# Zero points in packed 16-bit form, GpSimd makes the weights, VectorE takes half of the rescales

## The chip, the core and the metric

The kernel runs on one core of a Trainium2 chip. The metric is the device time of one execution in microseconds (us); of several runs the median is given. Besides that there is a profile of one execution, with the start and duration of every instruction of each engine: TensorE (PE, its weight loads PEld), VectorE (DVE), ScalarE (ACT), GpSimd (POOL) and SyncE (SP), which here only issues DMAs.

## What is computed

The input is 2 x 1024 rows of 1024 floats, 2048 rows in all. Each goes through a "macaron": half a feed-forward layer, a state-space layer (a long convolution along the 1024 values), and the same feed-forward layer again. Only the feed-forward layer matters here. Its three weight matrices are stored with 4 bits a value, eight to a 32-bit word, with a scale and a 4-bit zero point for every group of 128 input rows:

```python
w = (qw[:, None, :] >> shifts[None, :, None] & MAXQ).reshape(-1, qweight.shape[1])
z = ((qz[:, :, None] >> shifts[None, None, :] & MAXQ) + 1).reshape(qzeros.shape[0], -1)
W = (w - z[g_idx]) * scales[g_idx]
h = jax.nn.silu(xf @ Wg) * (xf @ Wu)
out = h @ Wd
```

Wg and Wu have 1024 rows (8 groups) and 2752 columns, Wd has 2752 rows (22 row blocks, 21 zero and scale rows) and 1024 columns. The result is `x + 0.5 * ffn(layernorm(x))`.

## The kernel before

**Jobs.** The rows are cut into four blocks b of 512. A feed-forward layer of one block is a job, and eight jobs (two per block) run one after the other. Only job 0 (j = 0) makes the weights: it unpacks them, writes them to DRAM as whole floats (`w_q`, `wd_q`), and all jobs load tiles from there. So nearly all that follows happens in job 0.

**Gate and up.** The 2752 columns are cut into units of 128 columns of gate or of up, and these into eight waves: five of six units, two of four, and a last one of five. For every wave eight steps g run over the groups of 128 input rows. In a step TensorE multiplies the weight tile (128 rows, 768 columns in a wave of six) with two parts of the normalized rows, a float part and a 16-bit rest, and adds both into the unit's accumulator in PSUM. Between two steps the accumulator is multiplied by the ratio of two scales (`scaled`, L521), so that it always stands in the scale of the next group; the last ratio is held by itself and goes into the gating. ScalarE does this (L523) or VectorE (L525). In `gate_up` L569 decides: ScalarE takes the even units, and in job 0 also the unit at place 1 of the wave, so four of six. After step 7 `gated` applies silu (L581, ScalarE), multiplies gate by up (hf, L584, VectorE), and splits the product into two parts on GpSimd: hh (L586) and hl (L588). There are two hf buffers and six accumulators.

**Down.** Two halves a of 512 output columns; in each 22 steps f over 128 rows with four accumulators. L628 decides who rescales: ScalarE takes c = 0 and 2, and in job 0 also c = 1 in three of four steps.

**Making the weights.** `fetch` (L407) loads a wave's packed words, `fetch_zeros` (L414) its zero points, one bf16 each, repeated for 16 partitions. `bytes_of` (L421) turns the words into two tiles of bytes with two VectorE instructions: the even nibbles by a mask, the odd ones by a shift and a mask. A byte then holds a nibble from 0 to 15. `dequantize` (L433) makes one of the eight tiles of a wave: VectorE takes every fourth byte, subtracts the zero point, and writes floats (L438); SP writes the tile to `w_q` (L442). For wave 0, GpSimd also copies each tile's first 16 partitions into the first weight tile by its own DMA (L441), so that step 0 need not go through DRAM. `fetch_down`, `split_down` and `dequantize_down` (L446 to L474) do the same for down, six blocks of eight tiles of 512 columns. The zero points themselves are unpacked once by `zero_points` (L257) and stored in DRAM. The dequantized tiles and the weight tiles of the steps share one ring of eight buffers (`wpool`), loads run four steps ahead (`AHEAD`).

**What sets the order.** Each engine works off its own list in order, and SP is one such list, with tile writes and weight loads mixed. The Tile framework's planner orders the instructions from the program text. Hooks set where in the text a piece of weight making stands (`first_weights`, L476: wave w's fetch 3 steps, its split 1 step ahead of its first tile, which stands 12 steps before the wave), and `in_order_of_writing` keeps some of them in the order written. `start` (L1277) writes out the beginning by hand: loads, zero points, moments of the rows, wave 0's tiles, transposes.

Of the kernel before, what the change touches and what calls it, by code (L numbers as in the profile page):

```python
# [12 lines left out]
I32 = mybir.dt.int32  # L13
U8 = mybir.dt.uint8
F32R = mybir.dt.float32r
# [21 lines left out]
STEPS = [(w, g) for w in range(len(WAVES)) for g in range(GK)]  # L37
NH = HID // 512
LIFT = 2.0**20
NST = 64  # L40
# [12 lines left out]
def macaron_s4_kernel(  # L53
# [180 lines left out]
    s_dn = const.tile([P, NC, GD], F32, tag="s_dn", name="s_dn")  # L234
    z_dram = dpool.tile([2 * GK, INTER], BF16, tag="z", name="z_dram")
    zd_dram = dpool.tile([GD, HID], BF16, tag="zd", name="zd_dram")
    ok = const.tile([P, 8], F32, tag="ok", name="ok")
# [19 lines left out]
    def zero_points(which, z):  # L257

        p, n = z.shape
        zi = t2(f"zi_{which}").bitcast(I32)[:p, : 8 * n]  # L260
        for k in range(8):
            nc.vector.tensor_scalar(
                zi.rearrange("p (a k) -> p k a", k=8)[:, k, :],
                z,
                4 * k,
                15,
                ALU.logical_shift_right,
                ALU.bitwise_and,
            )
        tab = t2(f"ztab_{which}").bitcast(BF16)[:p, : 8 * n]  # L270
        nc.vector.tensor_scalar(tab, zi, 1.0, None, ALU.add)
        dst, seg, queue = (zd_dram, SEGD, nc.sync) if which else (z_dram, SEG, nc.scalar)
        queue.dma_start(dst.rearrange("g (s n) -> (g s) n", s=seg), tab)
# [15 lines left out]
    def scales(k0, k1, row):  # L289
# [9 lines left out]
        if k1 == WIDE:  # L299
# [13 lines left out]
        nc.vector.tensor_scalar(  # L313
            own[:, :, GK - 1 :], s[:, :, GK - 1 :], 1.0 / LIFT, None, ALU.mult
        )

    def scales_down():
# [16 lines left out]
        )  # L334
        nc.vector.tensor_scalar(ratd[:, :, GD - 1 :], s_dn[:, :, GD - 1 :], 0.5, None, ALU.mult)

# [67 lines left out]
    packed = {}  # L404
    NIBBLES = 0x0F0F0F0F

# [7 lines left out]
    def fetch_zeros(w):  # L414
        z = t2(f"z_{w}").bitcast(BF16)[:, : width_of(w)]
        for own, i, lo, hi in columns(w):
            src = z_dram[GK * i : GK * i + GK, lo:hi]
            nc.sync.dma_start(z[:, own], src.unsqueeze(1).to_broadcast([GK, 16, hi - lo]))
        packed[w][1] = z

    def bytes_of(raw, even):  # L421

        nc.vector.tensor_scalar(even, raw, NIBBLES, None, ALU.bitwise_and)
        nc.vector.tensor_scalar(raw, raw, 4, NIBBLES, ALU.logical_shift_right, ALU.bitwise_and)
        view = lambda a: a.bitcast(U8).rearrange("p (n k) -> p k n", k=4)
        return view(even), view(raw)

    def split(w):
        raw = packed[w][0]
        even = t4(f"even_{w}").bitcast(I32)[:, : width_of(w)]  # L430
        packed[w][0] = bytes_of(raw, even)

    def dequantize(w, j):  # L433

        parts, z = packed[w]
        q = wpool.tile([P, width_of(w)], F32R, tag="w", name=f"q_{w}_{j}")
        src = parts[j % 2][:, j // 2, :]
        nc.vector.tensor_tensor(q, src, z, ALU.subtract)  # L438
        dst = w_q[w].rearrange("(r j) n -> j r n", j=8)[j]
        if w == 0:  # L440
            nc.gpsimd.dma_start(first_tile[j:P:8].bitcast(F32), q[: P // 8].bitcast(F32))  # L441
        nc.sync.dma_start(dst, q.bitcast(F32))  # L442
        if j == 7:
            packed.pop(w)

    def fetch_down(a, rt):  # L446
# [4 lines left out]
        nc.sync.dma_start(both[:, 0], down_qw[rt * P : rt * P + n, cs])  # L451
        z = t4(f"zd_{a}_{rt}").bitcast(BF16)[:n, :512]
        g0 = 8 * rt
# [8 lines left out]
    def split_down(a, rt):  # L462
        both, z = packed[a, rt]
        packed[a, rt] = (bytes_of(both[:, 0], both[:, 1]), z)

    def dequantize_down(a, rt, j):
        parts, z = packed[a, rt]
        n = z.shape[0]
        q = wpool.tile([P, 512], F32R, tag="w", name=f"qd_{a}_{rt}_{j}")[:n]
        nc.vector.tensor_tensor(q, parts[j % 2][:, j // 2, :], z, ALU.subtract)  # L470
        rows = wd_q[a][8 * P * rt : 8 * P * rt + 8 * n]
        nc.sync.dma_start(rows.rearrange("(r j) n -> j r n", j=8)[j], q.bitcast(F32))
        if j == 7:
            packed.pop((a, rt))  # L474

    def first_weights(up, dn, at):  # L476


        for w in range(1, len(WAVES)):
            s0 = 8 * w - 12  # L480
            if w > 1:
                both = lambda w=w: (fetch(w), fetch_zeros(w))
                at(up, s0 - 3, lambda both=both: in_order_of_writing(both, ET.SP))
                at(up, s0 - 1, lambda w=w: in_order_of_writing(lambda: split(w), ET.DVE))
            else:
                at(up, 0, lambda: in_order_of_writing(lambda: split(1), *STARTING))
            for j in range(8):
# [39 lines left out]
    def gate_up(j, b, hooks):  # L527
# [3 lines left out]
        for s, (wi, g) in enumerate(STEPS):  # L531
# [17 lines left out]
            for k, pos, done in turns:  # L549
# [18 lines left out]
                if g < GK - 1:  # L568
                    on_act = unit % 2 == 0 or (j == 0 and pos == 1)  # L569
                    if unit == 2 * WIDE:  # L570
# [35 lines left out]
    def down(j, b, hooks):  # L606
# [3 lines left out]
        for d, (a, f) in enumerate(steps):  # L610
# [7 lines left out]
            for c in range(4):  # L618
                for k, part in enumerate(reversed(h[f])):
# [7 lines left out]
                    )  # L627
                on_act = c % 2 == 0 or (j == 0 and c == 1 and f % 4 < 3)  # L628
                if f < GD - 1:
# [647 lines left out]
    def start():  # L1277
# [19 lines left out]
        moments(0, 1, then)  # L1297
        deviations(0, 1, -LIFT)
        for i in range(8):
            dequantize(0, i)  # L1300
# [100 lines left out]
```

## Time and profile before

| | us |
|---|---|
| Median of 3 runs (lowest to highest) | 2210.38 (2209.15 to 2211.67) |
| The profiled execution | 2211.56 |
| Its span, first to last instruction | 2209.8 |
| PE busy | 2121.7 (96%) |
| VectorE busy | 1703.2 (77%) |
| ScalarE busy | 1425.0 (64%) |
| GpSimd busy | 367.8 (17%) |
| First multiplication with weights | 28.75 |
| End of job 0, about | 333 |

A line of a group of instructions names the source line, the engine, the operation, output and inputs with their shapes, and the count; then the busy time and the mean duration in ns, then the idle time of the engine just ahead of them and what ended it. A line of the timeline gives start and duration in us, the same names, and in brackets the idle time ahead with its releaser. A busy PE is not a PE at its full pace: matmuls are pipelined, and the granted clock is given apart (1.00 is full). The pace is best read from the start of a step to the start of the next.

### The profile page before, as it was taken

Reading aid. Unit: us, or ns where it says so; the run is one execution under the profiler, and the core shown is the slowest. Engines: PE = TensorE matmul, PEld = TensorE weight load, DVE = VectorE, ACT = ScalarE, POOL = GpSimd, SP = SyncE. Lnnn points to the kernel's source line nnn. Section 1 sums busy time; section 2 is a strip of 40 time slices with the busy share of each in tenths; the row PEclk is TensorE's granted clock in tenths of the full one; section 3 lists DMA queues with packets and bytes.
Section 4 is the critical chain, followed back from the end, with each engine's and each line's share of the span. In section 5 each row is a group of like instructions: output and inputs, shape, how many; then the busy total and the mean of one; then the engine's idle time right before and its main releaser. Section 6 shows DMA issues by size and latency. Waiting matters only on the chain.

```text
span 2209.8 us, 27967 instructions
## 1 busy us (share of the span) xinstructions
PE 2121.7 (96%) x9524; PEld 1416.0 (64%) x9524; DVE 1703.2 (77%) x2803; ACT 1425.0 (64%) x2245; POOL 367.8 (17%) x389
## 2 busy tenths in 40 slices
PE   5888899999999999999999999999999999999998
PEld 3454575566867658655685558676586765865576
DVE  7777968777886877778877788867788677777776
ACT  5667776555764577666766667646776467766775
POOL 0222301121011220122102220112201122012210
PEclk9999999999999999999999999999999999999999
DMA  7778774434443545544655454434445354554443
GB/s 247 249 244 281 235 249 155 133 110 155 136 153 116 171 138 155 193 143 121 205 170 167 125 172 138 153 115 157 134 138 153 115 177 137 154 195 143 133 131 121
DMA packets 163669, 359.93 MB, mean 163 GB/s; under 512 B 22395, under 2 KB 27572, under 8 KB 163518
## 3 DMA queue, kind: packets, MB, share of 16 engines
q1 hardware_dynamic: 162670, 356.50, 50.7%
q8 instruction: 78, 1.28, 0.2%
q10 hardware_dynamic: 592, 1.16, 0.1%
q0 software_dynamic: 256, 0.39, 0.1%
q14 instruction: 73, 0.60, 0.1%
HBM read 306.86 MB, written 50.73 MB: 162 GB/s over the span
## 4 chain that ended last, share of the span: by engine, by line
PE 54%; issue 24%; DVE 4%; POOL 4%; DMA 1%; ACT 1%; SPq 0%; POOLq 0%; DVEq 0%; ACTq 0%
PE pg L558 32%; PE po L620 15%; PE pc L917 3%; POOL hl L588 3%; PE pc L898 1%; DVE hf L584 1%; POOL hh L586 1%; PE pb L641 1%; PE st L199 1%; DVE pg L525 1%; DMA wd<-wdq 1%; ACT g L581 0%; PE pt L199 0%; DVE po L525 0%; DVE qd L470 0%
## 5 line engine op out<-in xcount | busy, mean ns | idle before, releaser
L523 ACT ACTIVATE pg<-pg,rat 128x512 f32<-128x512 f32 x1264 | 799.7, 660 | 476.8 <-PE pg L558 471.9
L525 DVE TENSOR_TENSOR pg<-pg,rat 128x512 f32<-128x512 f32 x1144 | 764.7, 695 | 185.0 <-PE pg L558 180.1
L558 PE MATMUL pg<-xTh,w 128*128 128x512 f32 x2752 | 882.0, 445 | 22.0 <-DVE hf L584 12.4
L558 PE MATMUL pg<-xTl,w 128*128 128x512 f16 x2752 | 744.4, 384 | 19.0 <-DMA w<-wq 10.4
L558 PEld LDWEIGHTS pg<-xTh,w 128*128 128x128 f32 x2752 | 520.7, 190 | 208.2 <-DVE hf L584 24.3
L620 PE MATMUL po<-hl,wd 128*128 128x512 f32 x1344 | 539.4, 403 | 13.5 <-DVE po L525 8.9
L523 ACT ACTIVATE po<-po,ratd 128x512 f32<-128x512 f32 x670 | 437.6, 662 | 167.6 <-PE po L620 167.1
L620 PE MATMUL po<-hh,wd 128*128 128x512 f32 x1344 | 525.0, 393 | 0.0
L525 DVE TENSOR_TENSOR po<-po,ratd 128x512 f32<-128x512 f32 x610 | 421.0, 698 | 100.0 <-PE po L620 95.9
L558 PEld LDWEIGHTS <-w 128*128 128x128 bf16 x2752 | 227.6, 99 | 361.3 <-issue 183.8
L586 POOL CAST hh<-hf 128x512 fp32r<-128x512 f32 x168 | 109.6, 652 | 1535.9 <-DVE hf L584 1433.5
L620 PEld LDWEIGHTS po<-hl,wd 128*128 128x128 f32 x1344 | 252.8, 189 | 91.8 <-DVE po L525 22.3
L620 PEld LDWEIGHTS po<-hh,wd 128*128 128x128 f32 x1344 | 253.9, 189 | 46.1
L588 POOL TENSOR_TENSOR hl<-hf,hh 128x512 fp32r<-128x512 f32 x168 | 222.6, 1325 | 13.4
L584 DVE SCALAR_TENSOR_TENSOR hf<-pg,rat,g 128x512 f32<-128x512 f32 x168 | 121.9, 746 | 92.0 <-ACT g L581 59.4
L581 ACT ACTIVATE g<-pg,rat 128x512 f32<-128x512 f32 x168 | 106.9, 686 | 64.1 <-PE pg L558 63.8
L162 DVE BATCH_NORM_STATS2 stats<-x 128x6 f32<-128x512 f32 x96 | 63.6, 678 | 1.1
L199 PE MATMUL pt<-ident,xn 128*128 128x128 f32 x256 | 43.0, 285 | 11.1 <-ACT xn L1269 11.1
L222 DVE TENSOR_TENSOR xTl<-pt,xTh 128x512 f16<-128x512 f32 x56 | 38.3, 689 | 14.6 <-ACT xTh L221 14.4
L643 DVE TENSOR_TENSOR x<-x,pb 128x512 f32<-128x512 f32 x64 | 43.3, 680 | 6.3 <-PE pb L641 5.0
L199 PEld LDWEIGHTS pt<-ident,xn 128*128 128x128 f32 x256 | 33.4, 147 | 21.6 <-ACT xn L1269 12.8
L641 PE MATMUL pb<-ident,y 128*128 128x128 f32 x256 | 42.5, 279 | 3.5 <-DVE x L643 3.4
(151 smaller groups left out, 809.1 us busy)
## 6 DMA issues: line engine op xcount, KB each, us to landing
w<-wq SPq DMA_DIRECT2D x319, 384.0 KB
wd<-wdq SPq DMA_DIRECT2D x336, 256.0 KB
w<-wq SPq DMA_DIRECT2D x128, 256.0 KB
w<-wq SPq DMA_DIRECT2D x64, 320.0 KB
x<-in_L_attn_u_dram SPq DMA_DIRECT2D x30, 512.0 KB
wq<-q SPq DMA_DIRECT2D x40, 384.0 KB
wdq<-qd SPq DMA_DIRECT2D x32, 256.0 KB
xs<-x SPq DMA_DIRECT2D x16, 512.0 KB
```

What stands on the lines that cost most here:

```text
L162: nc.vector.bn_stats(stats[:, t, i, :], x[b][t][:, bass.ts(i, 512)])
L199: nc.tensor.transpose(ps[:, bass.ts(k, P)], n[:, bass.ts(k, P)], ident)
L523: nc.scalar.activation(dst, src, AF.Copy, scale=sc)
L525: nc.vector.tensor_tensor(dst, src, sc.to_broadcast([P, TB]), ALU.mult)
L558: nc.tensor.matmul(p, weights, (lo, hi)[k][:, g, :], start=(g == 0 and not done), stop=(g == GK - 1 and done), skip_group_check=True,)
L581: nc.scalar.activation(g, pg, AF.Silu, scale=rat[:, 2 * f, GK - 1 :])
L584: nc.vector.scalar_tensor_tensor(hf, pu, last, g, ALU.mult, ALU.mult)
L586: nc.gpsimd.tensor_copy(hi, hf)
L588: nc.gpsimd.tensor_tensor(lo, hf, hi.bitcast(F32), ALU.subtract)
L620: nc.tensor.matmul(ps[c], w[:, bass.ts(c, P)], part, start=(f == 0 and k == 0), stop=(f == NF - 1), skip_group_check=True,)
L641: nc.tensor.transpose(ps[:, bass.ts(c, P)], yT[a, c][:, bass.ts(t, P)], ident)
L917: nc.tensor.matmul(dst, lhsT, rhs, start=start, stop=stop, skip_group_check=True)
```

## The change

All arithmetic on zero points moves from the float subtraction of every tile to the packed bytes. The nibble is placed three bits higher in its byte (it counts eighths), the table holds 120 - 8z in both bytes of a 16-bit word, one 16-bit addition takes the zero points of two bytes at once, and an exclusive or with 0x8080 makes each byte a signed number, 8 (w - z - 1). What is left of the dequantization is a copy from signed byte to float, which GpSimd does; in wave 0 VectorE does six of the eight. The factor of 8 is taken out by the last scales. ScalarE's extra rescales in job 0 go to VectorE: each has half. The zero points in DRAM become a 32-bit word each (four equal bytes).

```diff
-        z = t2(f"z_{w}").bitcast(BF16)[:, : width_of(w)]
+        z = t4(f"z_{w}").bitcast(I32)[:, : width_of(w)]
...
-        tab = t2(f"ztab_{which}").bitcast(BF16)[:p, : 8 * n]
-        nc.vector.tensor_scalar(tab, zi, 1.0, None, ALU.add)
+        tab = t2(f"ztab_{which}").bitcast(I32)[:p, : 8 * n]
+        nc.vector.tensor_scalar(
+            tab.bitcast(U16).rearrange("p (n k) -> p n k", k=2),
+            zi.unsqueeze(2).to_broadcast([p, 8 * n, 2]),
+            -8.0 * 257,
+            120.0 * 257,
+            ALU.mult,
+            ALU.add,
+        )
...
-    NIBBLES = 0x0F0F0F0F
+    NIBBLES = 0x78787878
...
-        nc.vector.tensor_scalar(even, raw, NIBBLES, None, ALU.bitwise_and)
-        nc.vector.tensor_scalar(raw, raw, 4, NIBBLES, ALU.logical_shift_right, ALU.bitwise_and)
-        view = lambda a: a.bitcast(U8).rearrange("p (n k) -> p k n", k=4)
-        return view(even), view(raw)
+        nc.vector.tensor_scalar(even, raw, 3, NIBBLES, ALU.logical_shift_left, ALU.bitwise_and)
+        nc.vector.tensor_scalar(raw, raw, 1, NIBBLES, ALU.logical_shift_right, ALU.bitwise_and)
+        return even, raw
+
+    def signed(part, z):
+        both = part.bitcast(U16)
+        nc.vector.tensor_tensor(both, both, z.bitcast(U16), ALU.add)
+        nc.vector.tensor_scalar(both, both, 0x8080, None, ALU.bitwise_xor)
+        return part.bitcast(I8).rearrange("p (n k) -> p k n", k=4)
...
+    def take_zeros(w):
+        parts, z = packed[w]
+        packed[w] = [signed(part, z) for part in parts]
+
     def dequantize(w, j):
-        parts, z = packed[w]
         q = wpool.tile([P, width_of(w)], F32R, tag="w", name=f"q_{w}_{j}")
-        src = parts[j % 2][:, j // 2, :]
-        nc.vector.tensor_tensor(q, src, z, ALU.subtract)
+        engine = nc.vector if w == 0 and j % 3 < 2 else nc.gpsimd
+        engine.tensor_copy(q, packed[w][j % 2][:, j // 2, :])
...
-        packed[a, rt] = (bytes_of(both[:, 0], both[:, 1]), z)
+        packed[a, rt] = [signed(part, z) for part in bytes_of(both[:, 0], both[:, 1])]
...
-        nc.vector.tensor_tensor(q, parts[j % 2][:, j // 2, :], z, ALU.subtract)
+        nc.gpsimd.tensor_copy(q, src)
...
-                at(up, s0 - 1, lambda w=w: in_order_of_writing(lambda: split(w), ET.DVE))
+                both = lambda w=w: (split(w), take_zeros(w))
+                at(up, s0 - 1, lambda both=both: in_order_of_writing(both, ET.DVE))
...
-                    on_act = unit % 2 == 0 or (j == 0 and pos == 1)
+                    on_act = unit % 2 == 0
...
-                on_act = c % 2 == 0 or (j == 0 and c == 1 and f % 4 < 3)
+                on_act = c % 2 == 0
...
         deviations(0, 1, -LIFT)
+        take_zeros(0)
         for i in range(8):
             dequantize(0, i)
```

Not shown: wave 1's split and the zero points of down in the same form, and the last ratios with 1 / (8 LIFT) in L313 and 0.5 / 8 in L335.

## The prediction

> **What bounds the kernel now.** I read the busy times by stretch first, since an average over eight jobs hides the one that the change touches: all its instructions belong to job 0 (0 to 333 us). Columns: stretch and length, then busy us (count) of PE, PEld, DVE, ACT, POOL, the PE clock, DMA share, GB/s.
>
> ```profile
> 0.00:28.80 28.80, 5.81 (x24) 4.18 (x25) 21.87 (x64) 12.42 (x19) 4.76 (x15) 1.00 0.70 228
> 28.80:230.00 201.20, 173.88 (x732) 97.03 (x733) 154.00 (x231) 143.52 (x237) 47.67 (x40) 0.98 0.77 260
> 230.00:333.00 103.00, 92.89 (x388) 68.22 (x387) 81.22 (x136) 73.60 (x122) 21.34 (x19) 0.95 0.74 238
> 231.00:282.00 51.00, 46.03 (x191) 31.15 (x189) 48.48 (x85) 36.54 (x61) 20.42 (x17) 0.97 0.70 225
> ```
>
> PE sets the pace; it is idle for 28.8 us of startup and about 37 us after it. VectorE is busy 77 to 95% of the time. From 370 to 600 us PE is busy 98.6% of the time, so nothing is to be gained there.
>
> Next, the timeline of PE, gap by gap (start, duration, work, in brackets the idle time and what ended it). The large ones:
>
> ```profile
> 28.75 1.44 PE L558 MATMUL pg<-xTl,w 128*128 128x512 f16 x3 [1.81 <-DMA w<-q]
> 87.63 0.50 PE L558 MATMUL pg<-xTh,w 128*128 128x512 f32 x1 [2.58 <-DVE hf L584]
> 106.95 1.11 PE L558 MATMUL pg<-xTl,w 128*128 128x512 f16 x3 [2.67 <-DMA w<-wq]
> 144.95 0.79 PE L558 MATMUL pg<-xTh,w 128*128 128x512 f32 x1 [3.99 <-DVE hf L584]
> 236.34 0.50 PE L620 MATMUL po<-hl,wd 128*128 128x512 f32 x1 [1.64 <-DVE po L525]
> ```
>
> Sorted by releaser, the gaps between 28.8 and 333 us are: VectorE's gating (hf) 9.0, its rescales of pg 5.1 and po 4.6, together **18.7 us**; weight loads 10.4 (gate/up) and 3.7 (down), **14.1 us**; residual adds 2.7; ScalarE 1.6. The clock costs more: its share times length of each 10 us stretch gives a further 8.6 us (0.87, 0.83, 0.85 and 0.75 after the largest gaps).
>
> ScalarE has room: in waves with no gap it works 2.39 us of a 2.70 us step and then waits for PE. The weight gaps hang on VectorE too. The waits of SP's queue (us, times, longest) say
>
> ```profile
> SPq L442 <- DVE q L438: 78.9, 52, 4.6
> SPq L472 <- DVE qd L470: 42.2, 37, 4.9
> ```
>
> SP writes each dequantized tile and loads the next weights in one order, so a tile late on VectorE holds the loads behind it.
>
> **What the Trainium skill says.** "VectorE: DVE Perf Modes", the perf-mode tier table: a 16-bit tensor_tensor in SBUF runs at two elements a cycle, a one-source 16-bit operation at four, fp32 two-source at one. The trace agrees on the last and has no 16-bit packed operation. "SBUF — State Buffer", "SBUF: two separate sides": a VectorE operation with two SBUF inputs or in a two-port mode and a GpSimd operation exclude each other. The trace agrees: beside GpSimd's subtraction one dequantization took 2.02 us instead of 0.95.
>
> ```profile
> 60.53 2.02 DVE L438 TENSOR_TENSOR q<-even,z 128x768 fp32r<-128x768 uint8 x1
> 60.46 1.27 POOL L588 TENSOR_TENSOR hl<-hf,hh 128x512 fp32r<-128x512 f32 x1
> ```
>
> "GPSIMD Engine Reference", engine selection: one-input elementwise work runs at roughly line rate there. Undisturbed, its cast hh takes 0.61 us for 512 elements, its subtraction hl 1.27; no row has an 8-bit source.
>
> **The change in numbers.**
>
> *VectorE, removed:* 64 gate/up dequantizations, 21.6 + 19.6 + 7.0 + 5.5 + 5.4 + 3.3 = 62.4 us, and 48 down, 26.5 + 11.5 = 38.0: **100.4 us**.
>
> *VectorE, added:* (1) 56 gate/up rescales (one a step in seven of eight steps of eight waves) and 32 of down (15 + 1 in each half) come over from ScalarE: 88 x 0.695 = 61.2 us; ScalarE gives up 88 x 0.66 = 58 us that no gap needed. (2) 28 packed additions. At two a cycle, 1536 elements take as many cycles as the 768-element dequantization, 0.87 us start to start: 10 x 0.87 + 4 x 0.60 (1024) + 2 x 0.73 (1280) + 12 x 0.60 (down) = 19.8 us; at one a cycle about 38. (3) 28 XORs. At four a cycle 1536 cost as much as the 768-word shift (0.55 us, 0.47 start to start): 4.7 + 1.4 + 0.8 + 4.1 = 11.0; at two a cycle about 20. (4) Six copies of wave 0: 0.82 each by the cast hb (0.63 us for 512) = 4.9. (5) The zero tables twice as wide, 0.8. Sum 97.7, **net -2.7 us**; with both slower modes +24. I take the fast modes. So VectorE is not relieved in total: the work changes shape, from one or two dequantizations in every step to a block of 2 x 0.47 + 2 x 0.87 + 2 x 0.47 = 3.6 us once a wave.
>
> *GpSimd, added:* 34 copies of 768 at 0.92, 64 of 512 at 0.61, 8 of 640 at 0.76 = 76 us, scaled by width from the cast. With its 74 us that makes 150 of 333. An 8-bit source could be as dear as a two-input operation, 1.27 per 512: 159 us and 70% of the stretch.
>
> *DMA:* the zeros go as 32-bit words, 192 KB instead of 96 per piece, 2.2 MB more beside some 80 MB in job 0. Hidden by the 0.77 share; if not, 9 us at 250 GB/s. Constants (the factor 8 in L313, L335; mask, shifts) change no duration.
>
> *Startup.* VectorE has no gap from 6.1 to 23.5 us, so the wider table (+0.4) and wave 0's additions and XORs (2.7) move the first tile from 17.4 to about 20.6. Then six copies at 0.82 instead of eight at 0.87: the last at 24.6 instead of 23.5. GpSimd now does two copies between its eight DMA issues (0.48 each, about 0.1 between) and ends near 28.0 instead of 24.3. The first weights land 4.4 us later, near 32.4 instead of 28.7. But the second step is set by SP: eight 384 KB writes at 290 GB/s need 10.6 us, now from 20.7, and w_1 comes near 36 to 37 instead of 34.6. The first step's own slack takes part of it: **+2.5 us** (1 to 5.5).
>
> *Gaps from VectorE.* In ordinary steps it has three rescales at 0.65 in 2.70 us, as in later jobs, which run without gaps. At 82.5 to 88.2 two dequantizations (0.95 each) stood between hf and the next hf, at 137.8 to 144.3 three (one stretched to 1.78). They go, but the block lands on one step. Replayed on the new order in wave 1: additions and XORs lie between the rescales of units 7, 9 and 11; the last starts 6.4 us into the step instead of 2.9, PE has work until 5.5 and waits about 1.7; with the gating behind it the boundary costs 3.3, where 2.58 + 0.72 + 0.28 = 3.6 stood. Boundaries without scales cost about 1.5 each, down blocks (2 x 0.60 + 4 x 0.34 = 2.6) about 1. The 231 to 282 stretch is relieved most: 38 us of down dequantization against 12 of blocks and 22 of rescales. Altogether 18.7 becomes about 13: **-5.5**, and with fewer gaps over 2.5 us the clock gives back **-2**.
>
> *Gaps from weight loads.* A copy on GpSimd stands behind no rescale that waits for PE, so SP's 121 us of waits shrink; but it shares GpSimd with hh and hl (1.9 us a unit), and the tile ring of eight still holds it until PE frees a buffer. SP's order hardly moves: about one weight load in a wave now comes behind one more tile. 14.1 becomes 11.5: **-2.5**.
>
> Sum: +2.5 - 5.5 - 2 - 2.5 = -7.5. The profiled run took 2211.56 us (span 2209.8 and 1.76 around it), the median is 1.18 lower: 2210.38 - 7.5 = **2203 us**.
>
> **Rivals.** *A, the block is as dear as what went:* the gaps from VectorE stay at 18.7, loads gain 2, startup loses 2.5: about 2211, no difference. For it: VectorE's balance of -2.7. Against it: the two worst gaps had dequantizations in them. *B, slower: GpSimd too slow on bytes.* Place: tiles behind hh and hl, and the writes and loads behind them in SP's queue. At 2.0 us per 768 (against 0.92) the eight of a wave and its three units cost 8 x 2.0 + 3 x 1.9 = 21.7 of about 27 us, and the last tiles, due four steps before their wave, come some 1.5 us late at seven boundaries and in six down blocks: 13 x 1.5 = 19.5, less 5 gained on VectorE, plus 2.5 of startup, is +17: 2227. It decides from about 1.5 us a copy. Against it: the skill's line rate. *C, additions at one a cycle:* 18 us more in blocks, half of it on PE's path: -7.5 + 9, so 2212. *D, the pace of later jobs:* those run waves without gaps; the 37.1 + 8.6 = 46 us of gaps and clock halve, 2210.4 - 23 + 2.5 = 2190. That the change doesn't do what it says is ruled out by the order of instructions: the 112 subtractions are gone and their 106 GpSimd copies there.
>
> **How the numbers follow.** A change of 0.2% (4.4 us) is about what a measurement of this kernel can tell from none. Chances: forecast (2198 to 2206) 0.40, D 0.15, A 0.17, B 0.17, C 0.11. Faster: 0.40 + 0.15 = 0.55. A and C scatter about the kernel before: of their 0.28 I put 0.20 within 0.2% and 0.08 above it. Slower: 0.17 + 0.08 = 0.25. For 8 in 10 the range leaves out the far side of D (0.05) and most of B (0.13): 2189 to 2221. The likeliest case's own range is 2198 to 2206.
>
> **What would show it.** Right: rescales of 2.0 us a step on VectorE with a block of some 3.6 us a wave; 128x1536 additions at 0.95 and XORs at 0.55; GpSimd's 768 copies at 0.9 to 1.0; first matmul near 32; gaps after hf at wave boundaries shorter; SP's waits for q below 60 us. Wrong: additions at 1.7; copies above 1.5 with SP waiting on GpSimd; gaps at weight loads above 14; first matmul after 35 or before 30; or any change after 340 us beyond a shift.

## The result and the profile after

The changed kernel takes **2222.55 us** (median of 5 runs, 2217.4 to 2223.72) where the kernel before took 2211.67 (median of 5, 2209.15 to 2213.68): a ratio of **1.0039**, 95% interval 1.0029 to 1.005. (The ratio is an estimate from all runs; the quotient of these two medians, 1.0049, lies within its interval.) It is slower by 0.4%; I had forecast 0.3% faster. The profiled execution took 2217.4 us (span 2215.6), 5 us less than the median, so the profile holds about half of the loss and the experiments have to carry the rest.

Everything happens in the first job and in the way to the second. The last gating of job 0 starts 3.3 us later than before (233.4 for 230.1 us), the interval to that of job 1 is 2.5 us longer (318.0 for 315.5), and all six later intervals, here and in every kernel of this study, agree within 0.5 us.

Busy time by stretch of the changed kernel (columns as above: PE, PEld, DVE, ACT, POOL, PE clock, DMA share, GB/s):

```profile
28.80:230.00 201.20, 169.67 (x723) 94.37 (x723) 155.42 (x266) 113.94 (x178) 87.42 (x106) 0.99 0.80 266
230.00:333.00 103.00, 88.44 (x375) 65.77 (x374) 88.23 (x145) 57.25 (x90) 43.97 (x56) 0.97 0.74 244
231.00:282.00 51.00, 40.76 (x171) 28.99 (x170) 45.77 (x82) 26.69 (x43) 30.12 (x37) 0.97 0.66 218
```

ScalarE gave up 29.6 us in the first long stretch, GpSimd took on 39.7, and VectorE is where it was (155.4 for 154.0). The DMA share rises from 0.77 to 0.80, and PE does 4.2 us less work in that stretch.

The waits of PE in the changed kernel from 28.8 to 333 us (us in total, times, longest):

```profile
PE pg L582 <- DMA w<-wq: 16.4, 14, 2.6
PE po L644 <- DVE po L549: 7.7, 5, 2.4
PE pg L582 <- DMA w<-q: 5.5, 1, 5.5
PE pg L582 <- DVE hf L608: 4.9, 2, 3.1
PE pg L582 <- DVE pg L549: 4.7, 8, 1.4
PE po L644 <- DMA wd<-wdq: 3.3, 3, 2.5
```

and two of the same for the kernel before:

```profile
PE pg L558 <- DMA w<-wq: 10.4, 8, 2.7
PE pg L558 <- DVE hf L584: 9.0, 5, 4.0
```

The gating gaps (hf) fell from 9.0 to 4.9 us, as foreseen. The gaps before a weight tile of the first projections rose from 10.4 us to 16.4, and from 8 times to 14. On the timeline of PE, the start and two of the larger ones:

```profile
32.55 1.44 PE L582 MATMUL pg<-xTl,w 128*128 128x512 f16 x3 [5.46 <-DMA w<-q]
82.84 0.82 PE L582 MATMUL pg<-xTl,w 128*128 128x512 f16 x3 [2.30 <-DMA w<-wq]
111.12 0.82 PE L582 MATMUL pg<-xTl,w 128*128 128x512 f16 x3 [2.03 <-DMA w<-wq]
```

Where SP's queue stood still, 28.8 to 236 us, first in the changed kernel:

```profile
SPq L464 <- POOL q L460: 50.3, 28, 5.0
SPq L531 <- DMA wq<-q: 38.0, 14, 6.6
```

and in the kernel before, for the same stretch:

```profile
SPq L442 <- DVE q L438: 72.1, 47, 4.6
SPq L507 <- DMA wq<-q: 24.7, 10, 5.2
```

SP waits less for tiles, as expected, but longer with a weight load at its head (L531) whose source, a tile's write to DRAM, has not landed. The tiles come sooner; their writes land late. All eight tiles of a wave must be in DRAM before the wave's first load, which stands one step behind the last tile's write.

The order of SP's queue before wave 2 in the changed kernel (start, time of the issue):

```profile
72.48 0.80 SPq L464 DMA_DIRECT2D wq<-q  x1
73.36 0.45 SPq L422 DMA_DIRECT2D raw<-_L_ffn_gate_qweight_dram  x1
73.87 0.99 SPq L422 DMA_DIRECT2D raw<-in_L_ffn_up_qweight_dram  x1
74.92 1.23 SPq L429 DMA_DIRECT2D z<-z_dram  x2
76.25 0.47 SPq L531 DMA_DIRECT2D w<-wq  x1
76.82 0.38 SPq L464 DMA_DIRECT2D wq<-q  x1
77.69 0.32 SPq L531 DMA_DIRECT2D w<-wq  x1
80.24 0.35 SPq L464 DMA_DIRECT2D wq<-q  x1
86.08 0.35 SPq L531 DMA_DIRECT2D w<-wq  x1
```

The packed words and zero points of the next wave (73.4 to 76.2), now 768 KB instead of 576, are issued just ahead of this wave's last two tiles (76.82, 80.24), and the load behind them waits some 5.3 us, to 86.1. But PE didn't wait for that load, the first one of wave 2:

```profile
90.58 0.82 PE L582 MATMUL pg<-xTl,w 128*128 128x512 f16 x3
```

The two gaps shown above, at 82.84 and 111.12 us, stand before the seventh step of a wave. Its tile is the load issued directly behind the fetch (76.25, and 105.41 a wave later), before which SP did not wait. Gaps of this kind make 6.1 of the 16.4 us (3.6 of 10.4 before), gaps before the first tile of a wave 5.6 (3.2 before). So the fetch can be late for PE in two ways: for the load behind it, and for the write behind it. The Trainium skill, "DMA: Bandwidth & Descriptors", "Queues, rings and completion order", says that each DMA engine consumes the descriptors of a ring in ring order. The trace is in line with that: the load at 76.25 landed at 82.79, after the zero points (80.33 and 82.06). Whether it is the cause is for the experiments.

### The profile page after: what moved, and what is told of

It reads as the page before. It is cut to its first block, busy times and chain, and to the rows that moved or that the text cites. A ratio compares the mean times of both kernels' runs of the same rounds, so it can differ in the third digit from the quotient of the medians.

```text
span 2215.6 us, 28070 instructions
## 1 busy us (share of the span) xinstructions
PE 2118.1 (96%) x9524; PEld 1415.1 (64%) x9524; DVE 1713.2 (77%) x2841; ACT 1380.8 (62%) x2157; POOL 432.1 (20%) x495
## 4 chain that ended last, share of the span: by engine, by line
PE 57%; issue 24%; DVE 6%; POOL 5%; DMA 5%; ACT 1%; SPq 0%; ACTq 0%; POOLq 0%; DVEq 0%
PE pg L582 34%; PE po L644 16%; POOL hl L612 3%; PE pc L941 3%; DMA w<-wq 2%; DVE hf L608 2%; PE pc L922 1%; DVE pg L549 1%; POOL hh L610 1%; DMA z<-z_dram 1%; PE pb L665 1%; PE st L201 1%; DMA wq<-q 1%; DMA wd<-wdq 1%; PE pt L201 0%
## 5 line engine op out<-in xcount | busy, mean ns | idle before, releaser
L547 ACT ACTIVATE pg<-pg,rat 128x512 f32<-128x512 f32 x1208 | 771.4, 660 | 510.5 <-PE pg L582 507.2
L549 DVE TENSOR_TENSOR pg<-pg,rat 128x512 f32<-128x512 f32 x1200 | 801.7, 695 | 185.6 <-PE pg L582 180.9
L582 PE MATMUL pg<-xTh,w 128*128 128x512 f32 x2752 | 882.0, 445 | 16.4 <-DVE hf L608 8.8
L582 PE MATMUL pg<-xTl,w 128*128 128x512 f16 x2752 | 745.5, 384 | 30.4 <-DMA w<-wq 16.4
L547 ACT ACTIVATE po<-po,ratd 128x512 f32<-128x512 f32 x640 | 421.7, 662 | 182.7 <-PE po L644 182.7
L549 DVE TENSOR_TENSOR po<-po,ratd 128x512 f32<-128x512 f32 x640 | 441.4, 698 | 93.6 <-PE po L644 89.0
L610 POOL CAST hh<-hf 128x512 fp32r<-128x512 f32 x168 | 104.8, 624 | 1372.8 <-DVE hf L608 1325.7
L612 POOL TENSOR_TENSOR hl<-hf,hh 128x512 fp32r<-128x512 f32 x168 | 218.0, 1298 | 12.9
L201 PEld LDWEIGHTS pt<-ident,xn 128*128 128x128 f32 x256 | 33.5, 147 | 20.6 <-ACT xn L1293 12.2
L934 POOL TENSOR_TENSOR sums<-st 128x384 f32<-128x384 f32 x16 | 16.0, 1003 | 154.0 <-DVE st L968 154.0
```

Source lines behind the costliest of these rows:

```text
L201: nc.tensor.transpose(ps[:, bass.ts(k, P)], n[:, bass.ts(k, P)], ident)
L547: nc.scalar.activation(dst, src, AF.Copy, scale=sc)
L549: nc.vector.tensor_tensor(dst, src, sc.to_broadcast([P, TB]), ALU.mult)
L582: nc.tensor.matmul(p, weights, (lo, hi)[k][:, g, :], start=(g == 0 and not done), stop=(g == GK - 1 and done), skip_group_check=True,)
L610: nc.gpsimd.tensor_copy(hi, hf)
L612: nc.gpsimd.tensor_tensor(lo, hf, hi.bitcast(F32), ALU.subtract)
```

## The experiments

I had three theories from the two profiles. **Q**: GpSimd's place in the queues (its copies stand behind its own work on activations, and delay the start). **V**: VectorE's blocks and rescales. **Z**: the zero points, twice as many bytes and waited for. Later two more: **P**, it is the place of the fetch ahead of the last tile's write, and **B**, it is the sum of bytes wherever they stand. Each ratio is to runs of the kernel before on the same chip. Two columns come from one profile each: the gaps before weight matmuls of the first projections, 0 to 340 us, and the start of the last gating of job 0 with the interval to job 1's.

| kernel | ratio (95%) | median us | load gaps us (times) | job 0, interval |
|---|---|---|---|---|
| before | 1 | 2211.67 | 10.4 (8) | 230.1, 315.5 |
| changed | 1.0039 (1.0029-1.005) | 2222.55 | 16.4 (14) | 233.4, 318.0 |
| e1 wave 0 on VectorE | 1.0027 (1.0016-1.0038) | 2220.5 | 16.0 (13) | 234.4, 320.7 |
| e2 rescales back | 1.0039 (1.0027-1.0051) | 2222.52 | 19.3 (15) | 239.3, 317.0 |
| e3 all copies on VectorE | 1.0055 (1.0041-1.0068) | 2224.84 | 19.5 (10) | 238.9, 319.8 |
| e4 before, rescales moved | 1.0021 (1.0011-1.0031) | 2218.37 | 8.0 (9) | 230.7, 323.7 |
| e5 before, wide zeros | 1.0036 (1.0023-1.0049) | 2219.28 | 16.1 (11) | 236.6, 316.7 |
| e6 no additions | 1.0033 (1.0021-1.0046) | 2217.66 | 17.1 (14) | 231.5, 319.7 |
| e7 no zeros fetched | 0.9915 (0.9902-0.9928) | 2193.04 | 5.8 (6) | 215.7, 313.2 |
| e8 block in halves | 1.0054 (1.0041-1.0067) | 2223.3 | 16.8 (10) | 233.7, 323.3 |
| e9 changed, early fetch | 1.0005 (0.9997-1.0014) | 2214.54 | 15.0 (16) | 229.8, 320.1 |
| e10 before, early fetch | 0.9958 (0.9944-0.9971) | 2205.36 | 11.9 (11) | 225.7, 314.0 |
| e11 changed, shift 1 | 1.0007 (0.9999-1.0016) | 2215.32 | 16.4 (12) | 229.9, 321.9 |
| e12 before, shift 1 | 0.9966 (0.9952-0.9979) | 2206.73 | 7.1 (10) | 225.2, 315.9 |
| e13 before, other ring | 1.0006 (0.9998-1.0014) | 2213.56 | 14.0 (10) | 233.7, 316.5 |
| e14 changed, narrow zeros | 1.0035 (1.0022-1.0049) | 2221.76 | 10.8 (13) | 230.9, 326.3 |
| e15 before, byte zeros | 0.9989 (0.9981-0.9997) | 2210.46 | 8.8 (8) | 229.8, 314.9 |
| e16 before, e10 + e12 | 0.9951 (0.9938-0.9965) | 2201.97 | 9.1 (6) | 222.3, 313.9 |
| e17 e16 + byte zeros | 0.9945 (0.9927-0.9964) | 2203.66 | 8.5 (5) | 222.1, 315.8 |
| e18 changed, e9 + e11 | 1.0031 (1.0023-1.0039) | 2220.65 | 12.9 (8) | 233.8, 320.5 |

A single profile is one execution: it can stand 3 us from its kernel's median (e13's did) or 5 (the changed kernel's), so the ratios decide and the profiles say where.

### GpSimd's share: e1 and e3

```diff
-        engine = nc.vector if w == 0 and j % 3 < 2 else nc.gpsimd
+        engine = nc.vector if w == 0 else nc.gpsimd      # e1
+        engine = nc.vector                               # e3, down's copies too; rescales as in e2
```

> The changed kernel with one edit: all eight converting copies of wave 0 run on VectorE, none on GpSimd, so GpSimd does nothing but issue its eight DMAs there. VectorE's copies there take .55 us, so two more cost it 1.1 us. Theory Q (the loss is in the queues that feed the weight loads; the start is its first part): the eight DMA issues end about 1.5 to 2.5 us earlier than 27.1 us, the first matmul on a weight tile comes near 30.5 us (32.55 in the changed kernel, 28.75 in the kernel before), and the time falls by about 2 us, to some 2218 to 2221. Rival V (VectorE's rescales and blocks set the loss): the first matmul is earlier too, but the time does not follow by more than .5 us, because the accumulators of the first wave wait for VectorE's additions instead. Rival Z (the zero points' bytes and the wait for them): the start is held by the zero points and the first matmul moves by less than 1 us.

> The changed kernel with the rescales given back to ScalarE and every converting copy on VectorE, GpSimd left with its products and truncations of activations as in the kernel before. By the rows of both profiles VectorE does, against the kernel before, 100.4 us of subtractions less, 31 us of additions and exclusive ors more, and 74 copies of .37 to .55 us, about 40 us: 30 us less in all. Theory Q: the tiles no longer stand behind GpSimd's activations, so gaps before weight matmuls fall below those of the kernel before (10.4 us for the first projections); only the start stays 2 to 3 us late; the time is 2203 to 2210, faster than both kernels. Rival V expects the same direction but a smaller gain, as the blocks stay: 2210 to 2216. Rival Z (bytes): the tiles are early and the loads late all the same, because the zero points take DMA time: 2218 to 2223.

In e1 the first weight matmul did not move at all, although the last of GpSimd's eight issues came .7 us earlier:

```profile
32.55 1.44 PE L582 MATMUL pg<-xTl,w 128*128 128x512 f16 x3 [5.30 <-DMA w<-q]
```

So it isn't the end of the issues that sets the start. Its ratio, 1.0027, can't be told from the changed kernel's. In five kernels the first matmul follows the start of the *first* converted tile at a fixed distance: before 16.50 to 28.75 us, changed 20.43 to 32.55, e1 20.21 to 32.55, e6 16.79 to 29.24, e8 18.45 to 31.36, that is 12.1 to 12.9 us. Behind the first tile follow 3.5 MB of tiles (8 x 384 KB to DRAM, 8 x 48 KB to the first weight tile), and the DMA share is 0.96 and 1.00 in the two stretches of 4 us from 20 us on in the kernel before, 0.99 and 0.95 in those from 24 us on in the changed one. So the start reads as a DMA stretch that begins when the first tile is ready.

e3 was to be the fast version, with 30 us less work on VectorE than the kernel before and GpSimd free of tiles. It is no faster than the changed kernel or e2. In its profile the copies took VectorE 58.5 us and not 40, with additions and exclusive ors 98 in all, hardly less than the 100 of the subtractions; so it tests GpSimd's share, and not a lighter VectorE. Theory Q has fallen for the places where it was first put.

### VectorE's share: e2, e4, e6, e8

```diff
-                    on_act = unit % 2 == 0
+                    on_act = unit % 2 == 0 or (j == 0 and pos == 1)     # e2; e4: the reverse, in the kernel before
...
-        nc.vector.tensor_tensor(both, both, z.bitcast(U16), ALU.add)    # e6: both lines out
-        nc.vector.tensor_scalar(both, both, 0x8080, None, ALU.bitwise_xor)
```

(and in e2 and e4 the line of the down projection in the same way). e8 shifts, adds and flips the even half, then makes tiles 0, 2, 4, 6, then the odd half and tiles 1, 3, 5, 7.

> The changed kernel with the extra rescales of the first job given back to ScalarE, as in the kernel before: four of six accumulators on ScalarE in the waves of six, and five of eight in three steps of four of the down projection. VectorE loses about 61 us of work in the first 340 us. Rival V expects a gain: the gaps for accumulators fall from 17.0 us to at most 12, the VectorE blocks land earlier, and the time is 2213 to 2218. Theory Q expects no gain or a small loss: the tiles stand behind GpSimd, not VectorE, so the gaps before weight matmuls stay near 16 us for the first projections, and gaps released by ScalarE come back; 2221 to 2226. Rival Z expects the changed kernel's time within 1 us.

> The kernel before with the rescales alone moved as in the change: VectorE takes three of six and four of eight throughout the first job, and still makes every weight tile by a subtraction. VectorE has about 61 us more work in the first 340 us, on top of about 264, so it stands at nearly all of that time. Every theory expects a loss; rival V a large one, 15 to 30 us (2226 to 2241), with tiles late and gaps for accumulators at twice the 18.7 us. Theory Q expects 5 to 15 us, as tiles alone come late and the accumulators gain from a shorter queue on ScalarE. Under 3 us would say that VectorE had slack in the kernel before, and that neither the subtractions nor the rescales were worth moving.

> The changed kernel without its additions and exclusive ors: the zero points are fetched, but not subtracted and not waited for, so this part of the computation is left out. Rival V (the block of additions on VectorE is what was lost): about 31 us of VectorE work go, the start is 3.5 us earlier, gaps behind VectorE shrink, and the time falls by 8 to 14 us, below the kernel before (2208 to 2214). Theory Z: only the start and the waits for zero points go, 4 to 5 us (2217 to 2218), as the bytes still travel. Theory Q: the start's 3.5 us and little else, 2218 to 2220, because tiles stay behind GpSimd's activations.

> The changed kernel with its block cut in two: only the even half is shifted, added to and flipped before the first tile of a wave; the four even tiles come first, then the odd half, then the four odd tiles. The work is the same, its longest lump on VectorE falls from 3.6 to about 1.9 us, and at the start the first tile is ready 1.5 us earlier. Rival V (it is the lump, not the sum, that the accumulators pay for): the gaps for accumulators fall by 3 us or more and the start by 1.5, so 2217 to 2219. Theory Q: 1.5 us from the start, 2220 to 2222. Theory Z: 1.5 us from the start at most, and the gaps before weight matmuls stay near 16 us.

Giving the rescales back (e2) changes nothing: 1.0039 and 1.0039. Moving them alone in the kernel before (e4) costs 0.21%, and by its profile only in the down projection (interval 323.7 for 315.5), not in the first projections (230.7 for 230.1), where VectorE then worked 181 of 201 us. VectorE had that much slack there; I had expected e4 to lose 5 us at the least, and in the first projections it lost nothing.

Without additions and exclusive ors (e6), some 30 us of VectorE's busy time, the start is that of the kernel before within .5 us and the load gaps are still 17.1 us; ratio 1.0033, an interval that overlaps the changed kernel's and leaves no room for the 8 to 14 us that V expected. The halved block (e8) starts 1.2 us earlier and gains nothing. So neither the sum nor the lump on VectorE is what the time hangs on, and a start that is 1 to 3 us earlier mostly ends in a longer wait later. Theory V has fallen. In the down projection a block can be dear: on the timeline of VectorE in the changed kernel one takes 6.8 us instead of the 2.6 that I had summed, beside a GpSimd that was busy with the next rows (its one tile copy in this time took 0.8 us):

```profile
260.45 1.63 DVE L435 TENSOR_SCALAR rawd<-rawd 128x512 int32<-128x512 int32 x1 [0.29 <-DMA rawd<-_L_ffn_down_qweight_dram]
...
262.61 0.88 DVE L436 TENSOR_SCALAR rawd<-rawd 128x512 int32<-128x512 int32 x1
263.49 2.03 DVE L443 TENSOR_TENSOR rawd<-rawd,zd 128x1024 uint16<-128x1024 uint16 x2
265.44 2.24 DVE L444 TENSOR_SCALAR rawd<-rawd 128x1024 uint16<-128x1024 uint16 x2
```

```profile
263.90 1.07 POOL L220 CAST xTh<-turn 128x512 fp32r<-128x512 f32 x1
265.06 1.60 POOL L221 TENSOR_TENSOR xTl<-turn,xTh 128x512 f16<-128x512 f32 x1
```

That it cost time isn't shown: in e6, which has no additions and exclusive ors, PE waits 9.3 us for VectorE's rescales of po, more than the 7.7 of the changed kernel.

### The zero points' bytes: e5, e7, e13, e14, e15

```diff
-    z_dram = dpool.tile([2 * GK, INTER], BF16, tag="z", name="z_dram")
+    z_dram = dpool.tile([2 * GK, INTER], F32, tag="z", name="z_dram")    # e5; zd_dram and tables too
-        z = t2(f"z_{w}").bitcast(BF16)[:, : width_of(w)]
+        z = t4(f"z_{w}")[:, : width_of(w)]                               # e5
+        z = t4(f"z_{w}").bitcast(BF16)[:, : width_of(w)]                 # e13, nothing else
...
-            nc.sync.dma_start(z[:, own], src.unsqueeze(1).to_broadcast(...))   # e7, on top of e6; down too
...
-        nc.vector.tensor_tensor(both, both, z.bitcast(U16), ALU.add)
+        pairs = both.rearrange("p (n k) -> p n k", k=2)                  # e14: zeros of 16 bits each
+        nc.vector.tensor_tensor(pairs, pairs, z.unsqueeze(2).to_broadcast([*z.shape, 2]), ALU.add)
```

e15 is the kernel before with `U8` for `BF16` in tables, DRAM and tiles.

> The kernel before with one edit: the zero points stand in DRAM and in SBUF as 32-bit numbers, so every piece of them is 192 KB per 96 KB before, as in the change; what VectorE computes with them is unchanged. Theory Z (the bytes of the zero points crowd the weight transfers of the first job): the gaps before weight matmuls rise from 10.4 us toward 16 in the first projections and the time rises by 3 to 6 us, to 2216 to 2219. Theories Q and V: the bytes are hidden, the time is that of the kernel before within 1.5 us, and the first matmul stays at 28.8 us. A part of a microsecond may come from the wider table and from a subtraction that reads 32-bit zero points.

> As the run without additions and exclusive ors, and besides the zero points are not fetched at all (their tables are still made and written): subtraction and fetch are left out. The difference to that run is the price of the fetched bytes, 3.9 MB or so. Theory Z expects 4 to 8 us less than that run, with the gaps before weight matmuls down to 10 us or below. Theories Q and V expect at most 1.5 us less.

> The kernel before with its 16-bit zero points of gate and up placed in the large buffers (the ring of ten that holds the packed words) instead of the small ones; the bytes are unchanged. Theory W (bytes in the queue) expects no change: within 2 us of the kernel before. Theory R (the ring: the packed words now wait for buffers that the zero points hold) expects the 7 us that the wider zero points cost, 2217 to 2221.

> The changed kernel with one 16-bit zero point per column in DRAM and SBUF, as many bytes as in the kernel before; the addition reads each of them twice over a repeated axis, so I expect it to lose its fast rate and take 1.6 to 1.8 us for 1536 elements instead of .95, which makes the block of a wave 5.1 us instead of 3.6. Theory W (the bytes are the dearer part) expects 3 to 6 us less than the changed kernel, 2216 to 2220, in spite of the longer block. Theory L (the block is the dearer part) expects 3 to 10 us more, 2225 to 2232.

> The kernel before with zero points of one byte in DRAM and SBUF, half of its bytes; the subtraction reads two 8-bit sources and should keep its .95 us. Theory W, at 7 us for a doubling, expects 2 to 4 us less than the kernel before, 2209 to 2211; if what costs is the number of packets and not their bytes, nothing changes.

e5 is the main result: the kernel before, with its arithmetic, engines and rescales untouched and only its zero points twice as wide, loses 0.36%, as much as the whole change. Its subtractions take the same time (1.08 and .98 us for 768 columns in both), and its first matmul comes 1.2 us later. PE's waits in e5:

```profile
PE pg L558 <- DMA w<-wq: 16.1, 11, 5.0
```

e13 rules out the other thing that e5 altered, the buffers: with narrow zero points in the large ring the ratio is 1.0006, its interval holding 1 (its profiled execution, at 2216.5 us, is the third slowest of its 13 runs and shows 14.0 us of load gaps). e7 shows how much there is in total: without the fetch the time is 24.6 us below e6, which differs in nothing else. PE's waits in e7:

```profile
PE pg L578 <- DMA w<-wq: 5.8, 6, 2.6
```

With the fetch at its old place the load gaps follow the bytes: none 5.8 us, one byte 8.8, two bytes 8.0 to 14.0 (before, e4, e13, e14), four bytes 16.0 to 19.5 (changed, e1 to e3, e5, e6, e8). So, less neatly, do the gaps before the load directly behind a fetch of gate and up: none, 0.8, 0 to 3.6, and 2.6 to 7.2 us. In time e15's half gains only 0.11% and e14 gains nothing. In e14 the addition became slow, and the interval with the down projection is the longest of all (326.3); that its longer blocks took back what the bytes gave is likely, but not shown. So the price of the bytes is measured in the kernel before, and no run gives it for the changed one with its fast addition. The groups of e14 and, below, the same group of the changed kernel:

```profile
L445 DVE TENSOR_TENSOR even<-even,z 128x1536 uint16<-128x1536 uint16 x5 | 8.8, 1757 | 3.0 <-DMA z<-z_dram 3.0
```

```profile
L443 DVE TENSOR_TENSOR even<-even,z 128x1536 uint16<-128x1536 uint16 x5 | 4.8, 956 | 2.3 <-DMA z<-z_dram 2.3
```

The Trainium skill, "Advanced Engine Details and Errata", "2x-1p Requirements", asks for a unit step in the innermost dimension; the repeated one has step 0, and 1.757 us against .956 agrees.

### The place in the queue: e9 to e12, e16 to e18

```diff
-                at(up, s0 - 3, lambda both=both: in_order_of_writing(both, ET.SP))
+                at(up, max(0, s0 - 7), lambda both=both: in_order_of_writing(both, ET.SP))   # e9, e10
-            s0 = 8 * w - 12
+            s0 = 8 * w - 12 - (w > 2)                                                        # e11, e12
```

> The changed kernel with the packed words and zero points of waves 2 to 7 fetched seven steps ahead of their first tile instead of three (wave 2 at step 0). The bytes are the same, but they no longer enter SP's queue two steps ahead of the last tile of the wave before, whose write to DRAM the first loads of the next wave wait for. Theory P (the place in the queue: the zero points delay that write and so the load behind it) expects the gaps before weight matmuls to fall from 16 us to 10 or less and the time to 2208 to 2216. Theory B (the sum of bytes: the DMA engines have no time left in the first job) expects the changed kernel's time within 3 us, 2220 to 2226. Above 2226 would say that an early fetch takes buffers or a place that something else needed.

> The kernel before with the same early fetch. Here the zero points are half as wide. Theory P expects half of the gain or more, 2203 to 2209, and gaps before weight matmuls of at most 7 us instead of 10.4; theory B expects 2210 to 2214.

> The changed kernel with the fetch, block and tiles of waves 3 to 7 one step earlier, so that a step more lies between the write of a wave's last tile and the loads that wait for it; the order of transfers among them stays. Theory P expects less waiting at the turn of the waves, 4 to 8 us: 2215 to 2219. Theory B expects no gain, 2221 to 2224, as the same bytes must pass before the same matmuls.

> The kernel before with the same shift by one step of waves 3 to 7. Theory P expects 2 to 6 us less, 2206 to 2210; theory B expects 2211 to 2214.

> The kernel before with the early fetch (seven steps ahead) and the shift of waves 3 to 7 by one step together. If both act on the one wait, for the write of a wave's last tile, they overlap: 2202 to 2206. If they act on different waits they add: 2196 to 2201.

> The kernel before with the early fetch, the shift by one step, and zero points of one byte. If the bytes cost only where they stand in front of a wave's last tile, nothing is left to gain: 2201 to 2203. If they cost wherever they travel, 1.5 to 3 us less than with the two moves alone: 2198 to 2201.

> The changed kernel with the same early fetch and shift by one step, which took the kernel before to 2202. If the change loses only at the wait for a wave's last tile, the two now stand within 4 us (2202 to 2206; the later start alone is worth about 4). If its bytes and blocks cost it everywhere, it stays 7 to 10 us behind: 2209 to 2212.

Moving the same bytes four steps away from the write that the next wave waits for gains 0.34% in the changed kernel and 0.42% in the kernel before (e9, e10); setting fetch, block and tiles of waves 3 to 7 one step earlier, that write with them, gains 0.32% and 0.34% (e11, e12). No byte is saved and no instruction removed in any of the four. So the place of these transfers matters, and B alone can't account for it. SP's waits for that write, which had been 24.7 us (longest 5.2) before and 38.0 (longest 6.6) after, in e12 and e11:

```profile
SPq L507 <- DMA wq<-q: 15.4, 12, 2.6
```

```profile
SPq L531 <- DMA wq<-q: 16.9, 11, 5.0
```

In e10 it is 23.3 with 3.5 the longest, in e9 33.3 with 4.7: the early fetch shortens the longest waits, the shift most of them. Through which wait the gain comes is not shown: in e10 SP's waits for the write fell by 1.4 us only, and PE's load gaps are 11.9, with the hf gaps gone instead. By kind, the early fetch took gaps before the load directly behind a fetch (6.1 to 3.5 us in the changed kernel, 3.6 to 0.9 in the kernel before), the shift those before a wave's first tile (5.6 to 2.4, 3.2 to 0.9), and other load gaps came in their place. The first job of the kernel before became shorter, 225.7 and 225.2 us for 230.1; in the changed kernel (229.8 and 229.9 for 233.4) the two profiles show longer intervals behind it (320.1 and 321.9 for 318.0), and the gain rests on the ratios.

Nor is P shown to be what the change lost. The moves gain as much where the zero points have half the bytes: the two kernels stand 0.39% apart as they are, 0.47% with the early fetch, 0.41% with the shift. If the wider zero points cost time only by their place, the moves should have narrowed this distance. The run that would tell, the kernel before with wide zero points and both moves, was not made.

Both moves in the kernel before (e16) give 2201.97 us, ratio 0.9951: hardly more than one. In time the two overlap, though the gaps that they took are of two kinds. It is faster than both kernels and the version to keep. Byte-wide zero points on top (e17, 0.9945) can't be told from it.

In the changed kernel the two moves together (e18) give most of their gain back: 1.0031 where each alone had 1.0005 and 1.0007, so that it stands 0.8% behind e16, nearly 18 us. I had not expected that. The profile of e18 shows SP standing for 8.9 us at 88.6 to 98.1 us for a tile from GpSimd, which starts only when three units' products of activations are done. GpSimd in e18:

```profile
91.46 0.62 POOL L610 CAST hh<-hf 128x512 fp32r<-128x512 f32 x1 [7.15 <-DVE hf L608]
...
95.98 1.28 POOL L612 TENSOR_TENSOR hl<-hf,hh 128x512 fp32r<-128x512 f32 x1
97.20 0.83 POOL L460 CAST q<-even 128x768 fp32r<-128x768 int8 x1
```

and PE's gap that follows:

```profile
102.41 0.82 PE L582 MATMUL pg<-xTl,w 128*128 128x512 f16 x3 [3.64 <-DMA w<-wq]
```

That is theory Q's mechanism, at a turn of waves. It is read from one profile and was not tried by itself, and e11, with one wait of 6.5 us of the same kind, does not lose by it. Why e18 loses stays open.

## Why the prediction was wrong, by its steps

**The step that failed** is the one on DMA: "2.2 MB more beside some 80 MB in job 0. Hidden by the 0.77 share; if not, 9 us at 250 GB/s." The term was put at nothing, with the share for a reason. By e5 the doubled bytes alone cost the kernel before 0.36% of 2212 us, 8 us (5 to 11 by the interval), which is the 9 us that the prediction had written down and given no chance; that the two agree so well is partly luck, as 9 us were bytes over a mean rate. The share was read as 23% of room. But it is a mean over 200 us: in stretches of 4 us the DMA share of the kernel before goes from 0.24 to full, and the tile loaded directly behind a fetch is one that PE then waits for. Two things stay open: whether the bytes cost by their place in the queue or by their sum, and whether these 8 us are the same ones that the change lost, since it also has a later start (+4.1) and the moved rescales (0.21% alone, e4) and must win something back elsewhere. No rival held this mechanism; rival B named a loss by another road and twice the size (+17).

**Gaps from weight loads**, forecast 14.1 to 11.5 us, became 19.7 (16.4 and 3.3); above 14 was one of the prediction's own signs of being wrong. The forecast looked at one of SP's waits, that for tiles, and this did fall, from 78.9 us to 57.0 for gate and up (below 60, as foreseen). The other, for the landing of the writes, was in the view of SP's waits as well (24.7 us, third line) and was not worked with; it rose by 13.

**Gaps from VectorE**, forecast 18.7 to 13, became 17.3 (hf 4.9, pg 4.7, po 7.7). The hf part was right in kind and size, 9.0 to 4.9. The po part rose from 4.6 to 7.7 and was forecast to fall. One down block, sized at 2.6 us, took 6.8, but e6 without additions has 9.3 us of these gaps, so their cause stays open. More to the point, the arithmetic's move was worth nothing that can be seen: e2, which is e5 with additions and GpSimd copies in place of subtractions, has 1.0039 against 1.0036 (each within 0.13%), though 100 us of subtractions left VectorE and less than half of that came in blocks and copies. A start that is 2.6 us later (32.51 for 29.91) is part of this balance.

**Startup**, forecast +2.5 (1 to 5.5): the first matmul at 32.55 was forecast near 32.4, but the second step was to come at 36 to 37 and came at 38.7, so +4.1 of it was seen in full. The first tile came when forecast (its copy ended at 20.98, forecast 20.6). The reason given for the first matmul, the end of GpSimd's issues, was wrong (e1): in the five kernels above it follows the first tile.

**Clock**, forecast -2: in the profiled execution the share times length in the two stretches falls from 0.02 x 201 + 0.05 x 103 = 9.2 us to 5.1, so -4 there. The other four runs granted 0.991 to 0.993, as before, so over the runs there is little of it, and that the sign came right may be chance.

The sum for the profiled execution: +4.1 - 1.4 + 5.6 - 4.1 = +4.2, and its span grew by 5.8. **Prices of instructions** were right for gate and up: additions .951 and .956 us (.95 forecast), exclusive ors .554 and .656 (.55), GpSimd's 768-copies .828 and .939 (.92), so rivals B and C are out. In the down projection additions of 1024 took 1.09 and exclusive ors .67 on average, where those of gate and up took .69 and .42. VectorE's own six copies took .80 on average (.82 forecast), .55 undisturbed. A, no difference, has its VectorE gaps right (17.3 for 18.7) and, like the forecast, has the loads falling. D had assumed that the gaps would halve.

## What to carry to other kernels

A mean DMA share below 1 is no cover for more bytes: look for the transfer that is waited for, and ask what is queued ahead of it. Here an edit that moved 160 us of work between three engines was worth nothing that could be measured, the doubling of a small operand that came with it cost 8 us where it was tried by itself, and moving a fetch by a few steps, without changing any work, was worth 9. Before relieving an engine at 77% busy, follow the worst waits one step further back, from the load to the write that it reads and to the transfers ahead of both.

## What the runs showed of the hardware that was not expected

- An int8 to fp32r copy of 128x768 with a stride of 4 bytes took VectorE .55 us and GpSimd .83, undisturbed; beside GpSimd's copies VectorE's took up to 1.45.
- A 16-bit addition of 1536 elements took .956 us with packed operands and 1.757 with one operand repeated over an innermost step of 0.
- The 4.2 MB of broadcast zero points (by the issues 2752 KB for gate and up, 1344 KB for down) cost 24.6 us (e6 to e7), 170 GB/s, while the second half of them cost 8 us (e5), about 260 GB/s, the rate of that stretch. So the first half looks like the dearer one, though the two prices come from two kernels; its 18 issues of gate and up zero points occupy SP's queue for .57 us and more each, which is one candidate, untested.
- Another candidate: in the trace of the changed kernel the completion of the zero fetch at 74.92 us is counted up by eight late increments (79.94 to 80.33 us), that of the load at 76.25 by sixteen (81.64 to 82.79), and in the kernel before it is so for all 18 fetches of zero points of gate and up and for all 63 weight loads up to 240 us. It looks as if a fetch of eight rows, each repeated for 16 partitions, were shared by 8 of the 16 DMA engines, which it would then hold twice as long for its bytes. No run spreads it over more.
- The six intervals between later jobs repeat within 0.5 us over all twenty kernels, while the first job's end scatters by several us between runs of the same kernel.
